# Attention's units: SyncE's transfers issued in the order of the source

## The chip, the core and the metric

The kernel runs on one core of a Trainium2 chip. The core has a matrix engine (TensorE, in the profile PE for matmuls and PEld for weight loads), a vector engine (VectorE, DVE), a scalar engine (ScalarE, ACT), GpSimd (POOL), and SyncE (SP), which here does nothing but issue DMA transfers. Each engine works through its own list of instructions in a fixed order. An instruction that has to wait for a semaphore holds up everything behind it on the same engine, and that holds for SP too: a transfer that is not yet allowed to start keeps all later transfers on SP from being issued.

The metric is the device time of one execution in microseconds, as the median of several executions.

## What is computed

One transformer layer: cross attention with 16 heads of 32 numbers over 4 batches of 1024 tokens, and then a feed-forward layer in which 32 experts with 4 sets each pick one token of every group of 32.

```
x = x + attention(layernorm(x), ctx, ctx)      # causal without the diagonal, 16 heads
x = x + ffn(layernorm(x))
    logits = group of 32 tokens @ controller + tie
    perm = (logits == max over the group)
    inner = relu(perm-dispatched tokens @ f1 + bias)
    out = perm-returned (inner @ f2)
```

All matmuls of the attention are in float32, except those with masks and maxima, which are in bfloat16.

## The kernel before, in words

The attention is cut into 16 units: `b` counts the 4 batches, `hc` the 4 groups of 4 heads, and u = 4b + hc. Each unit runs 12 steps (8 key blocks, of which the first half of the queries sees 4 and the second half 8). In every step TensorE makes scores of unit u + 1 for their row maxima (`score_piece`, L388 to L415), scores of unit u turned round for the exponential (`key_block`, L457 to L488), and weighs the values (`weigh_values`, L508). DVE reduces the maxima and adds one half of the softmax sums, ACT does the exponentials, POOL blanks the diagonal blocks (`affine_select`, L484) and adds the other half of the sums (L504). Matmuls for keys, queries, values and output rows of other units (L274, L288, L307, L348) are put in between by a small planner in the source (`slot`, `choose`, `one_part`), which counts costs while the program is being written out.

The order of PE, DVE, ACT and POOL is that of the source: the whole attention and the routing behind it stand in one `tc.manual_schedule` over these four engines (L1120 to L1127). SP is not in that set. Its transfers go into the order that a scheduler finds at compile time by its own estimate of when each may start; transfers with nothing to wait for are therefore issued early.

The transfers that matter here, all on SP:

- `xt` (L204, 1 MB): half a batch of x for the layernorm's statistics of the next batch. There is one buffer, so half 1 waits until DVE has measured half 0 (L211, L212).
- `stats_dram<-ln_both` (L216): mean and 1/sigma of 512 tokens, written to DRAM in pieces of 4 bytes. It waits for POOL's power (L215). In the source it stands ahead of the load of half 1 (L219, L220).
- `both<-stats_dram` (L235, 512 KB): these statistics, read back and spread over all partitions.
- `xnT` (L231, 2 MB): the next batch of x, turned round.
- `inverse_dram<-rd`, then four `inverse<-inverse_dram` (L553, L556): the reciprocal sums of one half unit go to DRAM and come back spread over the partitions; DVE multiplies by them (`atT`, L538).
- `xr<-in_x_dram` (L327, 256 KB, three buffers): the residual of one row of 128 tokens. POOL adds the bias to it (L328), DVE adds the output row (L354), and SP stores it (`x_dram<-xr`, L355). `o_step` for row t asks for the residual of row t + 1 (L343, L344).
- `ct` (L106, 1 MB) and the weights (L99).

Behind the units, from L773 on, the routing of tokens begins, still inside the same function: `roots` (L817) makes 1/sigma of the rows, one DVE instruction and six powers on POOL (L819, L822), and `last_row` (L800) makes the rows of the last batch, whose residuals POOL prepares through L328 as well. The feed-forward layer follows.

Of the kernel before, what the change touches and what calls it, by code (L numbers as in the profile page):

```python
# [37 lines left out]
def attention_phase(  # L38
# [29 lines left out]
    def given(engine, cost):  # L68
        engine[0] = max(engine[0], now[0] + 0.2) + cost
        return engine[0]  # L70

    def scores_free():
        return max(read[0], read[1]) + 0.1

    def scores_given(work, engine, cost):
        now[0] = max(now[0], scores_free()) + work
        for _ in range(2):
            read.popleft()
            read.append(given(engine, cost))


    opool = ctx.enter_context(tc.tile_pool(name="attn_out", bufs=1))
# [42 lines left out]
    def finish(*names):  # L125
        for name in names:
            if name in pieces_left:
                cost, work = pieces_left.pop(name)
                work()
                given(dve, cost)  # L130

    def beside(budget):
        while aside and budget > 0:
            name = aside.popleft()
            if name in pieces_left:
                budget -= pieces_left[name][0]
                finish(name)
# [250 lines left out]
    def score_piece(u, k):  # L388
        i, c0, n = pieces[k]
        kT, qT = ks[u], qs[u]  # L390
        half = i // 4
        if (u, half) not in nms:
            nms[u, half] = spool.tile([P, 2, 4, R], F32, tag=f"nm{half}", name=f"nm_{u}_{half}")
        nm = nms[u, half]
        scs = [
            ps_s.tile([P, 2, HS], F32, tag="sc", name=f"sc_{u}_{k}_{g}") for g in range(2)
        ]
        diag = c0 + n == (i + 1) * P
        for r in range(R):
            rr = ds(r * HD, HD)  # L400
            nc.tensor.matmul(  # L401
                scs[r // 2][:, r % 2, :n], lhsT=qT[rr, ts(i, P)], rhs=kT[rr, ds(c0, n)],
                start=True, stop=not diag,
            )
        if diag:
            for r in range(R):
                nc.tensor.matmul(  # L407
                    scs[r // 2][:, r % 2, ds(n - P, P)], lhsT=ident16,
                    rhs=masks[0 if i == 0 else 1], start=False, stop=True,
                )  # L410
        scores_given(LARGE * n / HS + (0.45 if diag else 0.1), dve, 0.15 + 2.1e-3 * n)
        for g in range(2):
            nc.vector.tensor_reduce(  # L413
                nm[:, c0 // HS, i % 4, ts(g, 2)], scs[g][:, :, :n], AX.X, ALU.max, negate=True
            )  # L415
# [41 lines left out]
    def key_block(u, k):  # L457
# [13 lines left out]
        for r in range(R):  # L471
# [3 lines left out]
                start=False, stop=True,  # L475
            )
        scores_given(1.07 * n / HS + 0.22, act, 0.2 + 1.8e-3 * n)
        prs[u, k] = []
        for g in range(2):
# [151 lines left out]
    def one_part():  # L631
        if open_step[0] is None:
            open_step[0] = choose(True)
        if not advance(open_step[0]):
            open_step[0] = None
# [132 lines left out]
    while soon or fill or open_step[0]:  # L768
        one_part()
    beside(1e9)  # L770
    units.close()

# [323 lines left out]
@with_exitstack  # L1098
def xattn_ffn(ctx: ExitStack, tc, x, xT, ctxT, wqT, wkT, wvT, bv, woT, bo, ctrl, f1, biasT, f2, tie, out):
    nc = tc.nc  # L1100
    B, S, D = x.shape
    N = B * S
    cpool = ctx.enter_context(tc.tile_pool(name="consts", bufs=1))
    dram = ctx.enter_context(tc.tile_pool(name="scratch", bufs=1, space=bass.MemoryType.DRAM))
    ident = cpool.tile([P, P], F32, tag="ident", name="ident")
    make_identity(nc, ident)
    ident16 = cpool.tile([P, P], BF16, tag="ident16", name="ident16")
    nc.vector.tensor_copy(ident16, ident)
    mhalf = cpool.tile([P, 4], F32, tag="mhalf", name="mhalf")
    nc.gpsimd.memset(mhalf, -0.5)  # L1110
    consts = (ident, ident16, mhalf)
    x2_dram = dram.tile([N, D], F32, tag="x2d", name="x2_dram")
    stats_dram = dram.tile([2 * B, 2, S // 2], F32, tag="statsd", name="stats_dram")
    inverse_dram = dram.tile([2 * B * (D // P) * P, P], F32, tag="inversed", name="inverse_dram")
    routed = (
        dram.tile([N, D], F32, tag="xn2d", name="xn2_dram"),
        dram.tile([N, P], F32, tag="permd", name="perm_dram"),
        dram.tile([P, N], F32, tag="permTd", name="permT_dram"),
    )
    engines = {  # L1120
        mybir.EngineType.PE, mybir.EngineType.DVE, mybir.EngineType.Activation, mybir.EngineType.Pool
    }
    with tc.manual_schedule(engines=engines):
        attention_phase(
            tc, consts, x, xT, ctxT, wqT, wkT, wvT, bv, woT, bo, ctrl, tie,
            x2_dram, stats_dram, inverse_dram, routed,
        )  # L1127
    ffn_phase(tc, consts, x2_dram, routed, f1, biasT, f2, out)


# [36 lines left out]
```

## Time and profile before

| | |
|---|---|
| three executions | 1470.87, 1472.08, 1479.79 us (median 1472.08) |
| the profiled execution | 1467.71 us; its span on the core is 1465.9 us |
| granted TensorE clock, mean | 0.979 |
| DVE, ACT, POOL busy | 63%, 34%, 33% of the span |
| DMA engines busy by SP's queue | 25.0% |

The profiled execution was about 4 us faster than the median. By stretch of the span, from the table of busy times:

| stretch, us | what runs | PE busy, us | POOL busy, us | granted clock |
|---|---|---|---|---|
| 0 to 40 | first loads, first unit's projections | 27.34 | 5.05 | 1.00 |
| 40 to 1110 | attention | 1050.70 of 1070 | 420.14 | 1.00 |
| 1110 to 1150 | the last unit's end, routing begins | 29.22 of 40 | 24.59 | 0.77 |
| 1150 to 1240 | routing | 82.03 of 90 | 12.57 | 0.94 |
| 1240 to 1466 | feed-forward layer | 204.08 of 226 | 24.23 | 0.95 |

A line of a timeline reads: start in us, duration in us, engine, source line, operation, what it writes and reads, how many, and in brackets how long the engine sat idle before it and what ended the wait. SPq lines are transfers being issued; their time is that of issuing, not of the data. The chain of waits is read from the last instruction back, each piece being what the next one had to wait for.

### The profile page before, as it was taken

How to read it: one execution, taken by the hardware profiler on the slowest of the kernel's cores; microseconds unless marked ns; L12 is line 12 of the kernel's file. 1: busy time of each engine (PE TensorE's matmuls, PEld its weight loads, DVE VectorE, ACT ScalarE, POOL GpSimd, SP SyncE). 2: the span in 40 equal slices, each digit the busy share in tenths (PEclk: the TensorE clock that was granted, in tenths of full speed). 3: DMA queues.
4: the chain of work that ended last, by engine and by line, in shares of the span. 5: the costliest groups of instructions: out<-in, count | busy, mean ns of one | idle time of the engine just before them, and what ended most of it. 6: DMA issues, size and time to landing. Idle time of an engine off the chain costs nothing.

```text
span 1465.9 us, 31695 instructions
## 1 busy us (share of the span) xinstructions
PE 1393.4 (95%) x13704; PEld 733.0 (50%) x13704; DVE 927.5 (63%) x1377; ACT 502.4 (34%) x785; POOL 486.6 (33%) x557
## 2 busy tenths in 40 slices
PE   6999999999899999999999999999998898997997
PEld 4344544445344533543535344434443555887887
DVE  3666777656558586666666766565674464576666
ACT  2033333323132223332322232323334123645664
POOL 1034344333425253434343434333356320000122
PEclk9999999999999999999999999999999797899999
DMA  8011202001230210011212000010112679657554
GB/s 298 26 48 35 77 24 67 20 1 41 57 105 30 89 53 10 11 56 40 86 44 62 30 19 11 10 38 10 39 39 76 222 245 327 178 164 235 184 165 146
DMA packets 96972, 125.25 MB, mean 85 GB/s; under 512 B 12992, under 2 KB 54336, under 8 KB 96704
## 3 DMA queue, kind: packets, MB, share of 16 engines
q1 hardware_dynamic: 94272, 114.84, 25.0%
q0 software_dynamic: 2560, 8.39, 1.9%
q8 instruction: 107, 1.75, 0.5%
q14 instruction: 33, 0.27, 0.1%
HBM read 91.78 MB, written 31.42 MB: 84 GB/s over the span
## 4 chain that ended last, share of the span: by engine, by line
PE 80%; issue 6%; DVE 6%; DMA 3%; POOL 2%; ACT 1%; SPq 0%; POOLq 0%; DVEq 0%; ACTq 0%
PE sc L401 12%; PE st L467 10%; PE av L517 9%; PE pq L288 8%; PE pk L274 8%; PE pv L307 8%; PE po L348 5%; PE pd L957 3%; PE sc L407 3%; DVE nm L413 2%; PE pi L976 2%; PE st L473 2%; PE po L808 2%; PE pl L845 2%; PE pd L543 2%
## 5 line engine op out<-in xcount | busy, mean ns | idle before, releaser
L413 DVE TENSOR_REDUCE nm<-sc 128x2 f32<-128x1024 f32 (+3 forms) x384 | 349.2, 951 | 264.3 <-PE sc L407 179.1
L481 ACT ACTIVATE pr<-st 128x1024 f32<-128x1024 f32 (+3 forms) x384 | 290.4, 808 | 584.3 <-PE st L473 563.1
L484 POOL TENSOR_SCALAR_AFFINE_SELECT pr<-pr 128x256 f32<-128x256 f32 x256 | 122.2, 487 | 383.5 <-ACT pr L481 381.4
L504 POOL TENSOR_TENSOR acc<-acc,pr 128x1024 f32<-128x1024 f32 (+3 forms) x128 | 209.4, 1636 | 93.3 <-ACT pr L481 85.6
L401 PE MATMUL sc<-kT,qT 32*128 32x512 f32 (+3 forms) x1536 | 206.3, 531 | 8.6 <-ACT pr L481 4.9
L467 PE MATMUL st<-qT,kT 32*128 32x512 f32 (+3 forms) x1536 | 191.1, 534 | 4.7 <-DVE nm L413 4.6
L517 PE MATMUL av<-pr,v 128*32 128x512 f32 (+3 forms) x1536 | 166.4, 501 | 7.8 <-POOL pr L484 4.3
L274 PE MATMUL pk<-ct,w_k 128*128 128x512 f32 x256 | 131.0, 629 | 9.9 <-DMA w_k<-in_wkT_dram 9.2
L307 PEld LDWEIGHTS pv<-w_v,ct 128*128 128x128 f32 x1024 | 119.5, 192 | 34.6 <-issue 24.7
L467 PEld LDWEIGHTS st<-qT,kT 32*128 32x128 f32 x1536 | 68.6, 183 | 127.6 <-issue 99.9
L401 PEld LDWEIGHTS sc<-kT,qT 32*128 32x128 f32 x1536 | 74.4, 183 | 115.4 <-issue 50.6
L504 DVE TENSOR_TENSOR acc<-acc,pr 128x1024 f32<-128x1024 f32 (+3 forms) x128 | 126.2, 986 | 9.2 <-POOL pr L484 8.9
L307 PE MATMUL pv<-w_v,ct 128*128 128x128 f32 x1024 | 131.4, 281 | 0.2 <-DMA w_v<-in_wvT_dram 0.2
L288 PE MATMUL pq<-xnT,w_q 128*128 128x512 f32 x256 | 127.3, 616 | 1.5 <-ACT xnT L194 1.5
L501 POOL TENSOR_TENSOR acc<-pr,pr 128x768 f32<-128x768 f32 (+1 forms) x32 | 66.7, 2085 | 161.5 <-ACT pr L481 161.5
L1078 POOL DMA_DIRECT2D out_dram<-xr x32 | 24.2, 757 | 238.8 <-DVE xr L1077 237.6
L348 PE MATMUL po<-w_o,atT 128*128 128x512 f32 x192 | 95.5, 616 | 0.0
L517 PEld LDWEIGHTS av<-pr,v 128*32 128x32 f32 x1536 | 32.0, 108 | 95.0 <-issue 67.2
L274 PEld LDWEIGHTS pk<-ct,w_k 128*128 128x128 f32 x256 | 43.9, 194 | 68.9 <-issue 55.0
L473 PE MATMUL st<-mxT,ones 32*128 32x512 bf16 (+3 forms) x768 | 74.6, 322 | 0.3 <-DVE mxT L444 0.3
L288 PEld LDWEIGHTS pq<-xnT,w_q 128*128 128x128 f32 x256 | 43.0, 189 | 52.9 <-issue 46.2
L967 DVE COPY disp<-pd 128x512 f32<-128x512 f32 x64 | 41.2, 686 | 33.0 <-PE pd L957 30.1
(101 smaller groups left out, 1499.7 us busy)
## 6 DMA issues: line engine op xcount, KB each, us to landing
ct<-in_ctxT_dram SPq DMA_DIRECT2D x8, 1024.0 KB, 5.1
xt<-in_x_dram SPq DMA_DIRECT2D x8, 1024.0 KB, 5.4
xr<-in_x_dram SPq DMA_DIRECT2D x32, 256.0 KB, 2.7
xn_dram<-x SPq DMA_DIRECT2D x8, 1024.0 KB, 5.7
xn<-xn_dram SPq DMA_DIRECT2D x8, 1024.0 KB, 5.5
f<-in_f_dram SPq DMA_DIRECT2D x16, 512.0 KB, 4.5
f<-in_f_dram SPq DMA_DIRECT2D x32, 256.0 KB, 5.9
xr<-x_dram SPq DMA_DIRECT2D x32, 256.0 KB, 4.7
```

Source lines behind the costliest of these rows:

```text
L274: nc.tensor.matmul(pk, lhsT=weights["k"][:, c, ts(hc, P)], rhs=cts[b, half][:, c, :], start=(c == 0), stop=(c == NC - 1),)
L288: nc.tensor.matmul(pq, lhsT=weights["q"][:, c, ts(hc, P)], rhs=xnTs[b][:, c, ts(half, HS)], start=(c == 0), stop=(c == NC - 1),)
L307: nc.tensor.matmul(pv[:, t, :], lhsT=cts[b, half][:, c, ts(t, P)], rhs=weights["v"][:, c, ts(hc, P)], start=(c == 0), stop=(c == NC - 1),)
L348: nc.tensor.matmul(po, lhsT=atTs[b * NC + c][:, ts(t, P)], rhs=weights["o"][:, c, :], start=(c == 0), stop=(c == NC - 1),)
L401: nc.tensor.matmul(scs[r // 2][:, r % 2, :n], lhsT=qT[rr, ts(i, P)], rhs=kT[rr, ds(c0, n)], start=True, stop=not diag,)
L413: nc.vector.tensor_reduce(nm[:, c0 // HS, i % 4, ts(g, 2)], scs[g][:, :, :n], AX.X, ALU.max, negate=True)
L467: nc.tensor.matmul(scs[r // 2][:, r % 2, :n], lhsT=kT[rr, ts(j, P)], rhs=qT[rr, ds(h * HS + q0, n)], start=True, stop=False,)
L473: nc.tensor.matmul(scs[r // 2][:, r % 2, :n], lhsT=ones16[rr, :], rhs=mxT[rr, ds(q0, n)], start=False, stop=True,)
L481: nc.scalar.activation(pr[:, :, :n], scs[g][:, :, :n], AF.Exp)
L484: nc.gpsimd.affine_select(out=d, in_=d, compare_op=ALU.is_ge, fill=0.0, base=0 if j == 0 else -1, pattern=[[0, 2], [P + 1, P]], channel_mu ...
L504: engine.tensor_tensor(acc, acc, pr[:, :, :n], ALU.add)
L517: nc.tensor.matmul(avs[u, h][rr, q0:], lhsT=vs[u][:, j, rr], rhs=pr[r // 2][:, r % 2, : HS - q0], start=(j == 0), stop=(j == last),)
```

## The change

SP joins the set of engines whose order is that of the source, for the units only; behind the units the routing stands in a `manual_schedule` of its own, without SP, as before.

```diff
@@ in attention_phase, ahead of the pools
+    compute = {
+        mybir.EngineType.PE, mybir.EngineType.DVE, mybir.EngineType.Activation, mybir.EngineType.Pool
+    }
+    ordered = ExitStack()
+    ordered.enter_context(tc.manual_schedule(engines=compute | {mybir.EngineType.SP}))
@@ behind the last unit
     beside(1e9)
+    ordered.close()
     units.close()
+    ctx.enter_context(tc.manual_schedule(engines=compute))
@@ in xattn_ffn
-    engines = {
-        mybir.EngineType.PE, mybir.EngineType.DVE, mybir.EngineType.Activation, mybir.EngineType.Pool
-    }
-    with tc.manual_schedule(engines=engines):
-        attention_phase(
...
+    attention_phase(
```

No instruction is added or taken away, but the built program differs in its order in three places.

PE and ACT keep every instruction where it was. SP's 380 transfers are the same ones, in another order up to the end of the units. Around the point where batch 3 is prepared (b is the batch whose rows are being finished):

```
before                                 after
xt half 1 (batch 3)                    stats_dram half 0
stats_dram half 0                      xt half 1 (batch 3)
both half 0                            inverse_dram, 4 inverse
inverse_dram, 4 inverse                stats_dram half 1
stats_dram half 1                      xr row 1
x_dram row 0, xr row 3                 x_dram row 0, ct, xr row 2
x_dram row 1, xr row 4                 x_dram row 1, xr row 3
x_dram row 2, inverse_dram, ...        x_dram row 2, inverse_dram, 4 inverse
xr row 5, xnT                          xnT, both half 0
```

So a residual's load stands one row later than before (that of row t + 2 behind the store of row t, where it was that of row t + 3), the loads of rows 1 and 2, which stood in the batch before, stand just ahead of their use, half 1 of `xt` stands behind the write of the statistics instead of ahead of it, and `both` stands behind `xnT`. The same holds for batches 1 and 2, where batch 1 has no rows to finish. At the start, `xt` half 1 now stands ahead of `w_o`, and `ct` of batch 1 and the first three residuals leave the front of the queue for the place of their use.

Third, the routing's instructions are no longer tied behind the units' by one common schedule, and the built program has some of them earlier. On DVE one instruction moves: `roots` (L819) stands behind the last row's moments of batch 2, ahead of the reciprocal of unit 15's first half, instead of behind the last `atT`. On POOL nine move: the residual of row 0 of batch 3 now stands ahead of unit 15's first diagonal block, and this is the stretch in the middle of unit 15:

```
before                                 after
acc (steps 4, 5)                       acc (steps 4, 5)
acc (step 6)                           rstd x6, xr row 1
acc (step 7)                           acc (step 6) 
affine_select (step 8)  ...            xr row 2
... acc (step 11)                      acc (step 7) 
xr row 0, rstd x6                      affine_select (step 8)  ...
xr row 1, xr row 2                     ... acc (step 11) 
```

More of the change, by code (lines that the diff above doesn't have):

```diff
@@ L1119, in xattn_ffn @@
     )
-    engines = {
-        mybir.EngineType.PE, mybir.EngineType.DVE, mybir.EngineType.Activation, mybir.EngineType.Pool
-    }
-    with tc.manual_schedule(engines=engines):
-        attention_phase(
-            tc, consts, x, xT, ctxT, wqT, wkT, wvT, bv, woT, bo, ctrl, tie,
-            x2_dram, stats_dram, inverse_dram, routed,
-        )
+    attention_phase(
+        tc, consts, x, xT, ctxT, wqT, wkT, wvT, bv, woT, bo, ctrl, tie,
+        x2_dram, stats_dram, inverse_dram, routed,
+    )
     ffn_phase(tc, consts, x2_dram, routed, f1, biasT, f2, out)
```

## The prediction

> **What bounds the kernel now.** I read the page first, then the chain of waits, then the waits of SP's queue, and then timelines of single places. TensorE is busy nearly all the time, and nearly all of the chain that ended last is its work:
>
> ```profile
> PE 1393.4 (95%) x13704; PEld 733.0 (50%) x13704; DVE 927.5 (63%) x1377; ACT 502.4 (34%) x785; POOL 486.6 (33%) x557
> PE 80%; issue 6%; DVE 6%; DMA 3%; POOL 2%; ACT 1%; SPq 0%; POOLq 0%; DVEq 0%; ACTq 0%
> ```
>
> So a better order of transfers can win little: in the attention (40 to 1110 us) PE is idle for 19 us in all. One place with a transfer in the chain is large:
>
> ```profile
> 356.79 11.34 DMA inverse_dram<-rd
> ...
> 369.44 3.18 DMA inverse<-inverse_dram
> ...
> 372.74 0.69 DVE atT L538
> ...
> 375.42 0.62 PE st L467
> ```
>
> A write of 64 KB takes 11.34 us here; the usual one takes 1.5 us (median of the DMA table). PE idles 4.62 us ahead of 375.42. Ahead of that write on SP stands the write of the statistics (issued at 356.11). What such a write does to its followers is seen best where nothing else moves:
>
> ```profile
> 677.77 0.38 SPq L216 DMA_DIRECT2D stats_dram<-ln_both  x1
> 682.12 0.34 SPq L355 DMA_DIRECT2D x_dram<-xr  x1
> 689.03 0.34 SPq L327 DMA_DIRECT2D xr<-in_x_dram  x1
> ```
>
> The load at 689.03 waits for the store of 682.12 to land (its buffer). That store takes 6.9 us instead of its usual 2.0, and ends 11.3 us after the statistics were issued. The other places agree: 356.11 to 368.13 is 12.0 us, and 395.58 to 408.00, the same pair in batch 2, is 12.4 us. So: what is queued behind a write of the statistics completes some 11.3 us after its issue. Each time the program before puts only writes, or nothing urgent, into that shadow. The change puts reads there that DVE and POOL wait for.
>
> **The change part by part.**
>
> *Start.* `xt` half 1 moves ahead of `w_o`. It is issued at 20.45 in both orders, as it waits for DVE's `xn`. DVE first reads it at 26.54, but PE meets its result only at 32.48, straight behind busy matmuls: a gain of some us there stays under PE. `w_o` is needed at the first output row, at 392.8, and `ct` and the early residuals at hundreds of us too: 0. If that cover were gone the loss would be one load, 5.4 us.
>
> *Residuals one row later.* Some 20 loads now follow the store two rows before. A load takes 2.7 us to land, rows are about 6 us apart, and the load no longer waits for a store that has just been issued (before: 2 to 4 us of SP each time). POOL adds the bias at a row's start (L328), so it may wait up to about 1 us and has slack at 39% load in this stretch. 0; bounds -1 and +3.
>
> *`xt` half 1 behind the statistics, batches 1 and 3.* Before, it is issued 1.5 us ahead of the statistics, and is in SBUF in time:
>
> ```profile
> 92.39 0.38 SPq L204 DMA_DIRECT2D xt<-in_x_dram  x1
> 93.91 0.37 SPq L216 DMA_DIRECT2D stats_dram<-ln_both  x1
> ```
> ```profile
> 99.81 0.68 DVE L211 BATCH_NORM_STATS2 ln_stats<-xt 128x6 f32<-128x512 f32 x1
> ...
> 102.04 0.96 DVE L550 RECIPROCAL rd<-pd 128x128 f32<-128x128 f32 x1 [1.33 <-PE pd L543]
> 103.50 2.35 DVE L413 TENSOR_REDUCE nm<-sc 128x2 f32<-128x1024 f32 x2 [0.50 <-PE sc L401]
> ```
>
> [...]The row of an undisturbed `xt` load is 5.4 us: issued at 94.3 it would land at 99.7, just in time, cost 0. [...]No read follows the statistics in this trace, so it can't show it. [...]With 1 MB to move, four times the store's, I put the landing at 12.0 us behind the issue: 105.9. DVE is then 6.1 us late; its idle 1.33 us absorbs some; the reductions at 103.50, which PE's next scores wait for, come 4.8 us late: **+4.8**. In batch 3 the statistics go at 642.60, `xt` lands at 654.6, DVE reads it at 649.92: 4.7 late, 0.6 absorbed ahead of the reciprocal at 652.73: **+4.1**. Bounds: 0 each by the row of the lone load; by full serial work (11.3 + 5.4 us) +9 each.
>
> *Batch 2.* The same, but there DVE waits for the inverse first. Write and loads of the inverse now stand behind `xt` and no longer with 512 KB of `both` between them: write complete at 356.11 + 12.2 = 368.3, last load issued 1.4 later, landing 2.0 later: 371.7 instead of 372.62: **-0.9**. Bounds -4.6 (the whole wait) and +4.
>
> *Residual of row 1 behind the second statistics, batches 2 and 3.* Before it was loaded long ahead. Now it completes as that store did, 11.3 us after the issue, at 689.1 in the copy shown above:
>
> ```profile
> 678.94 1.26 POOL L328 TENSOR_TENSOR xr<-xr,bo_sb 128x512 f32<-128x512 f32 x1
> 681.88 1.22 POOL L484 TENSOR_SCALAR_AFFINE_SELECT pr<-pr 128x256 f32<-128x256 f32 x2 [1.68 <-ACT pr L481]
> ```
> ```profile
> 684.21 1.20 DVE L504 TENSOR_TENSOR acc<-acc,pr 128x256 f32<-128x256 f32 x1
> ...
> 688.26 0.69 DVE L354 TENSOR_TENSOR xr<-po,xr 128x512 f32<-128x512 f32 x1 [2.08 <-PE po L348]
> ```
>
> POOL stands at L328 until 689.1, adds until 690.4, and only then blanks the diagonal of 681.88 (its first half done at 690.8). DVE's sum at 684.21 reads it: 6.6 late. DVE's 2.08 idle us ahead of L354 absorb part; PE's next row at 689.03 needs L354 to free its PSUM bank: **+4.4**, and the same again at 395.58: **+4.4**. Bounds: 0 by the lone load's 2.7 us, +6.6 by serial work.
>
> *POOL's own order in unit 15.* This needs no assumption on DMA:
>
> ```profile
> 1119.80 2.35 POOL L504 TENSOR_TENSOR acc<-acc,pr 128x1024 f32<-128x1024 f32 x1 [5.46 <-ACT pr L481]
> 1124.87 2.42 POOL L504 TENSOR_TENSOR acc<-acc,pr 128x1024 f32<-128x1024 f32 x1 [2.72 <-ACT pr L481]
> 1127.25 0.41 POOL L484 TENSOR_SCALAR_AFFINE_SELECT pr<-pr 128x256 f32<-128x256 f32 x1
> ...
> 1139.16 1.27 POOL L328 TENSOR_TENSOR xr<-xr,bo_sb 128x512 f32<-128x512 f32 x1
> 1144.98 6.17 POOL L822 TENSOR_TENSOR rstd<-rstd,mhalf 128x4 f32<-128x4 f32 x6 [4.55 <-DVE rstd L819]
> 1151.13 2.48 POOL L328 TENSOR_TENSOR xr<-xr,bo_sb 128x512 f32<-128x512 f32 x2
> ```
>
> The six powers and two residuals move ahead of the first two lines. DVE's last moments of batch 2 end at 1119.69, `rstd` at 1119.9, so on POOL: 6.2 of powers to 1126.1, residual to 1127.3, sum to 1129.7, residual to 1130.9, sum to 1133.4. The blanking of 1127.25 comes 6.1 us late, and from there to 1139 POOL is nearly without a gap and PE and DVE wait for it: +5.8. The residual of row 0, ahead of unit 15's first diagonal, lands at 1099.40 (its load is at 1096.88 either way), so the blanking of 1097.05 starts at 1100.7: 3.6 late, 2.8 after slack. Back comes the first power ahead of the routing's first tokens (1144.98 to 1146.03): -1.2. Sum **+7.4**; bounds 0 (POOL catches up) and +10.
>
> Sum: 4.8 + 4.1 - 0.9 + 4.4 + 4.4 + 7.4 = **+24.2 us**. Against the profiled execution's own 1467.7 that is 1491.9; the median of the runs shown stands 4.4 higher, so 1496.3, said as **1496 us**.
>
> **The rivals.**
>
> *The reads are not held* (the side of no change): a transfer into SBUF behind the statistics completes in its own 2.7 or 5.4 us. For it: [...]no read is shown late. Against it: [...]three late writes. Then both +4.4 and the +4.8 and +4.1 go, batch 2 gains 3 to 4.6, and POOL's 7.4 remains: +3 to +4, with the residuals' 1 us and less gain +8: 1475 to 1480, inside 1%. It decides where a read lands less than 6 us after the statistics' issue.
>
> *POOL absorbs its nine instructions*: the sums of unit 15 wait for ACT for 5.46 and 2.72 us, so some room is there. Against: the powers cannot start before 1119.9. Then 24.2 - 7.4 = +16.8: 1489.
>
> *Full serial work*: 9 + 9 + 6.6 + 6.6 + 4 + 7.4 = +42: 1514.
>
> *The order does what it is for*: SP's blocked head no longer delays others. All waits of DVE for the inverse are 18.9 us, 7 times, and most are the round trip itself; only the 4.6 us above reach PE. A gain over 1% is not in reach of that.
>
> **How the numbers follow.** Forecast 0.61, POOL absorbs 0.11, reads free 0.20, serial 0.06, a gain 0.02. One per cent, 14.7 us, is about what a measurement here tells from no change. Slower: the forecast, serial, and somewhat over half of the POOL case (1489 is at 1.14%), 0.73. Within 1%: reads free, the rest of the POOL case, 0.25. Faster: 0.02. The range goes from 1477, into the free reads, to 1504 (forecast with both `xt` landings 2 us later and 3 us more at rows); below and above it lie about 2 in 10.
>
> **What will show it.** SP's timeline: L204 directly behind L216 in batches 1 to 3. DVE: a wait of 5 to 6 us for DMA `xt` ahead of L211 near 100 us and near 655. POOL: a wait of about 10 us for DMA `xr` near 397 and 685, with PE's gap of 4 us behind it. Unit 15: `rstd` on POOL before the sums. It is wrong if those loads land within 6 us, or if PE has no gap behind unit 15's blanking.

## The result, and the profile after

| | before | after |
|---|---|---|
| median of the runs made together | 1471.5 us (1467.5 to 1479.8) | 1515.1 us (1514.7 to 1523.0) |
| ratio to before, 95% interval | | 1.030 (1.025 to 1.036) |
| profiled execution: time, span | 1467.7, 1465.9 us | 1523.0, 1521.3 us |
| mean granted TensorE clock of that execution | 0.979 | 0.961 |

The change costs 43.6 us, where 24.2 were forecast. The kernel before has only four runs here; beside the later experiments its medians are 1476.8 to 1479.2 us, so the cost may be nearer to 36 to 38 us, near the low end of the interval. The profiled execution after is 8 us longer than its median. Some 6.6 us come before 95 us, where nothing new waits and only the granted clock is lower: its record has two stretches of 6.83 us at half clock, from 61.67 and 75.33, which the profile before lacks. PE's longest pauses there are 0.35 and 0.79 us.

The page after, first its busy times and then the engines' shares of the chain that ended last:

```profile
PE 1414.3 (93%) x13704; PEld 740.3 (49%) x13704; DVE 928.4 (61%) x1377; ACT 502.6 (33%) x785; POOL 486.3 (32%) x557
PE 75%; issue 7%; DMA 6%; DVE 6%; POOL 4%; ACT 1%; SPq 0%; POOLq 0%; DVEq 0%; ACTq 0%
```

The work is the same (the counts are), the chain has moved: DMA from 3% to 6%, POOL from 2% to 4%. That PE is "busy" 21 us longer with the same 13704 matmuls already says that they ran slower.

Lines moved by 7: the load of `xt` is now L211, the write of the statistics L223, the residual's load L334, POOL's bias addition L335. SP's timeline in batch 1 (start, duration):

```profile
100.49 0.37 SPq L223 DMA_DIRECT2D stats_dram<-ln_both  x1
100.95 0.53 SPq L211 DMA_DIRECT2D xt<-in_x_dram  x1
```

and DVE's, with its idle time ahead of the instruction in brackets:

```profile
116.20 0.69 DVE L218 BATCH_NORM_STATS2 ln_stats<-xt 128x6 f32<-128x512 f32 x1 [9.71 <-DMA xt<-in_x_dram]
...
117.87 2.29 DVE L420 TENSOR_REDUCE nm<-sc 128x2 f32<-128x1024 f32 x2
```

The read is behind the write, as the order says. DVE waits 9.71 us for it, and the reductions of L420, which free TensorE's scores, stand behind. Whether the read was held or merely slow is seen in the view of the DMA over 98 to 120 us (40 slices of 0.55 us; the last rows give the size and the time from issue to landing):

```profile
DMA  0000005200004521351995422699963000000130
GB/s 0 0 0 0 0 0 5 2 0 0 0 0 22 26 22 15 30 19 11 63 22 15 11 11 34 153 317 384 361 246 138 26 11 0 0 0 0 29 90 0
...
xt<-in_x_dram SPq DMA_DIRECT2D x1, 1024.0 KB, 15.2
...
stats_dram<-ln_both SPq DMA_DIRECT2D x1, 4.0 KB, 11.6
```

The 4 KB of statistics (1024 pieces of 4 bytes) take 11.6 us to land. For some 7 us of that the 1 MB behind them crawls at 11 to 30 GB/s with single slices above it; its bulk moves at up to 384 GB/s when the write is nearly done. So the read's data itself waits. 15.2 us is 11.6 plus most of a load (5.4 us alone). Why the data waits, no run here shows.

In batch 2 the inverse stands behind both:

```profile
373.25 0.38 SPq L223 DMA_DIRECT2D stats_dram<-ln_both  x1
373.75 0.52 SPq L211 DMA_DIRECT2D xt<-in_x_dram  x1
374.31 0.50 SPq L560 DMA_DIRECT2D inverse_dram<-rd  x1
388.74 1.71 SPq L563 DMA_DIRECT2D inverse<-inverse_dram  x4
```

The read-back of the inverse waits for its write, which lands 15.4 us after the statistics' issue; the forecast had 12.2.

Row 1's residual in batch 3, on SP, then POOL, DVE and PE:

```profile
715.62 0.38 SPq L223 DMA_DIRECT2D stats_dram<-ln_both  x1
716.04 0.58 SPq L334 DMA_DIRECT2D xr<-in_x_dram  x1
```
```profile
727.74 1.26 POOL L335 TENSOR_TENSOR xr<-xr,bo_sb 128x512 f32<-128x512 f32 x1 [10.91 <-DMA xr<-in_x_dram]
728.96 0.77 POOL L491 TENSOR_SCALAR_AFFINE_SELECT pr<-pr 128x256 f32<-128x256 f32 x2
```
```profile
729.40 0.60 DVE L511 TENSOR_TENSOR acc<-acc,pr 128x256 f32<-128x256 f32 x1 [7.40 <-POOL pr L491]
```
```profile
724.09 1.98 PE L355 MATMUL po<-w_o,atT 128*128 128x512 f32 x4
...
731.92 3.78 PE L355 MATMUL po<-w_o,atT 128*128 128x512 f32 x4 [4.88 <-DVE xr L361]
```

This is the chain of the forecast link by link: POOL at its bias addition, the blanking behind it, DVE's sum, PE's row. The last line holds one more thing. Its four matmuls take 3.78 us, where those of the row before take 1.98. They run at about half speed. The view by windows shows it around the first stall (columns: window, length, busy time and instructions of PE, PEld, DVE, ACT, POOL; then the granted clock, DMA share, GB/s):

```profile
108.00:110.50 2.50, 2.50 (x30) 0.73 (x20) 0.00 (x0) 1.09 (x2) 1.33 (x1) 1.00 0.76 26
110.50:113.00 2.50, 0.91 (x4) 0.08 (x2) 0.00 (x0) 0.00 (x0) 1.02 (x1) 0.97 0.51 135
113.00:115.50 2.50, 0.00 (x0) 0.00 (x0) 0.00 (x0) 0.00 (x0) 0.00 (x0) 0.50 0.60 231
...
118.00:120.50 2.50, 1.41 (x6) 0.65 (x8) 2.50 (x3) 0.00 (x0) 0.00 (x0) 0.50 0.09 26
120.50:123.00 2.50, 2.50 (x16) 1.09 (x12) 1.21 (x2) 1.77 (x2) 0.00 (x0) 0.50 0.49 105
123.00:125.50 2.50, 2.50 (x18) 0.54 (x12) 1.61 (x3) 0.17 (x1) 2.19 (x1) 0.50 0.03 7
125.50:128.00 2.50, 2.50 (x21) 1.18 (x18) 2.47 (x4) 0.39 (x1) 0.16 (x1) 0.79 0.00 0
128.00:130.50 2.50, 2.50 (x22) 1.62 (x21) 0.16 (x1) 1.55 (x2) 0.81 (x1) 1.00 0.00 0
```

PE stops at 111.4 and starts again at 119.1. The granted clock is halved from 112.9 to 126.5, so PE works at half clock for 7.4 us. Each of the five stalls of the changed kernel ahead of unit 15 has such a tail; they last from 4.8 to 7.4 us. In the record of the granted clock the five slow stretches last 13.65, 10.24, 6.83, 10.24 and 6.83 us, which is four, three and two times 3.41, the shortest such stretch in this execution (near 1038 us). They begin 1.4 to 4.2 us after PE's last matmul (whose end is modelled in the profile). What sets these times, no run here shows.

Starts of the same matmul in the two profiled executions, compared in quiet places between the events, give what each event costs with its tail. The stall is the jump at the event itself:

| event | forecast | jump | with what follows it |
|---|---|---|---|
| before 95 us (clock alone, this execution) | 0 | | 6.6 |
| `xt`, batch 1 | 4.8 | 7.7 | 10.6 |
| `xt` and inverse, batch 2 | -0.9 | 2.3 | 2.0 |
| row 1, batch 2 | 4.4 | 5.0 | 7.9 |
| `xt`, batch 3 | 4.1 | 7.2 | 10.8 |
| row 1, batch 3 | 4.4 | 5.0 | 7.8 |
| 900 us to the end (unit 15) | 7.4 | | 9.8 |
| sum, us | 24.2 | | 55.4 |

55.4 is the difference of the two spans. Without the first row it is 48.8, and the medians differ by 43.6. The tails of the five stalls can be estimated from the clock as well: the half clock lasts for 30.5 us in all from where PE starts again, and for 5.3 us behind the one such stall before, which at half speed (the 3.78 us against 1.98 above) makes (30.5 - 5.3) / 2 = 12.6 us; the table has 39.1 - 27.2 = 11.9. The last row holds more than unit 15: 1.6 us come near 1038 us, where the clock dips once for 3.41 us, and 1.3 us in the feed-forward layer. Unit 15 itself, compared at 1090 and 1160 us of the kernel before, costs 7.0, with 20.5 us at half clock in both kernels.

### The profile page after: what moved, and what is told of

It is laid out like the page before. It is cut to its first block, busy times and chain, and to the rows that moved or that the text cites. A ratio compares the mean times of both kernels' runs of the same rounds, so it can differ in the third digit from the quotient of the medians.

```text
span 1521.3 us, 31670 instructions
## 1 busy us (share of the span) xinstructions
PE 1414.3 (93%) x13704; PEld 740.3 (49%) x13704; DVE 928.4 (61%) x1377; ACT 502.6 (33%) x785; POOL 486.3 (32%) x557
## 4 chain that ended last, share of the span: by engine, by line
PE 75%; issue 7%; DMA 6%; DVE 6%; POOL 4%; ACT 1%; SPq 0%; POOLq 0%; DVEq 0%; ACTq 0%
PE sc L408 11%; PE st L474 10%; PE pk L281 8%; PE pq L295 8%; PE av L524 8%; PE pv L314 7%; PE po L355 5%; PE pd L966 3%; DVE nm L420 3%; PE sc L414 2%; PE pi L985 2%; DMA xt<-in_x_dram 2%; PE st L480 2%; PE pl L854 2%; PE po L817 2%
## 5 line engine op out<-in xcount | busy, mean ns | idle before, releaser
L420 DVE TENSOR_REDUCE nm<-sc 128x2 f32<-128x1024 f32 (+3 forms) x384 | 349.3, 951 | 276.2 <-PE sc L414 184.6
L474 PE MATMUL st<-qT,kT 32*128 32x512 f32 (+3 forms) x1536 | 197.2, 545 | 21.3 <-DVE nm L420 21.2
L355 PE MATMUL po<-w_o,atT 128*128 128x512 f32 x192 | 99.2, 636 | 9.7 <-DVE xr L361 9.7
L1087 POOL DMA_DIRECT2D out_dram<-xr x32 | 24.2, 757 | 240.1 <-DVE xr L1086 238.9
L335 POOL TENSOR_TENSOR xr<-xr,bo_sb 128x512 f32<-128x512 f32 x32 | 40.9, 1281 | 90.5 <-DMA xr<-in_x_dram 63.5
```

What stands on the lines that cost most here:

```text
L355: nc.tensor.matmul(po, lhsT=atTs[b * NC + c][:, ts(t, P)], rhs=weights["o"][:, c, :], start=(c == 0), stop=(c == NC - 1),)
L420: nc.vector.tensor_reduce(nm[:, c0 // HS, i % 4, ts(g, 2)], scs[g][:, :, :n], AX.X, ALU.max, negate=True)
L474: nc.tensor.matmul(scs[r // 2][:, r % 2, :n], lhsT=kT[rr, ts(j, P)], rhs=qT[rr, ds(h * HS + q0, n)], start=True, stop=False,)
```

## The experiments

Each kernel was timed beside the kernel before on the same chip; ratios are to that. Times alone scatter by 1.3% here (the kernel before: 1467 to 1487 us in 29 runs made beside the last two kernels). Each run's span times its mean granted clock scatters by far less (1435 to 1443 in the same 29), so most of the scatter is clock. I use both: this product for the waits (a microsecond at half clock counts half in it, whether PE works or waits), and what is left, span times (1 - clock), for the clock. The end of a stall, which passes at half clock too, is therefore shared between the two.

**Undoing the parts, one by one and together.** First, `xt` half 1 ahead of the statistics:

```diff
             if i == 3:
...
+                if half == 0:
+                    load(1)
                 nc.sync.dma_start(
                     stats_dram[2 * b + half].rearrange("s (i p) -> p s i", p=P), mv
                 )
-                if half == 0:
-                    load(1)
```

> The changed kernel, but the load of xt half 1 is issued ahead of the first write of the statistics instead of behind it (batches 1 to 3); nothing else differs. Theory A (the read is held behind the statistics, and each stall of TensorE is followed by a stretch at a lower clock): the three stalls of 7.7, 2.3 and 6.7 us that the comparison of the traces shows go, and with them some 2 us each of slower clock: 1515 falls by 20 us (16 to 26), to about 1495; xt lands about 6 us after its issue; granted clock about 1.00 between 100 and 140 us. Theory B (the late xt costs what its stalls are, no clock loss): -16.7 at most. Theory C (the loss sits in the rows and in unit 15, the DVE wait for xt is absorbed): less than -6.

Second, row 1's residual with row 0's (POOL's bias addition for row 1 moves with it):

```diff
             if hc == 0:
                 load_residual(b - 1, 0)
+                if more:
+                    load_residual(b - 1, 1)
...
-        if ahead:
+        if ahead and ahead not in residuals:
             load_residual(*ahead)
```

> The changed kernel, but the residual of output row 1 is loaded together with that of row 0, ahead of the statistics of the next batch (batches 1 and 2's rows, loaded in batches 2 and 3); nothing else differs. Theory A: the two stalls of about 5 us at POOL's bias addition near 407 and 689 us go, with 2 to 4 us each of slower clock behind them: -14 us (-10 to -18). Theory B (stalls alone): -10. Theory C (POOL's wait is absorbed by slack): less than -4. POOL's wait for xr of about 10 us ahead of its bias addition should be gone.

Third, the four computing engines under one hand-written order around the whole phase, as before, and SP alone added within the units:

```diff
-    ordered.enter_context(tc.manual_schedule(engines=compute | {mybir.EngineType.SP}))
+    ordered.enter_context(tc.manual_schedule(engines={mybir.EngineType.SP}))
...
-    ctx.enter_context(tc.manual_schedule(engines=compute))
...
+    with tc.manual_schedule(engines=engines):
+        attention_phase(
```

> The changed kernel with SyncE in the new order, but with POOL and DVE in the order of the kernel before (nine instructions on POOL and one on DVE move back; SyncE's order is that of the changed kernel to the instruction). Theory A: unit 15's blanking is no longer behind the powers and two residuals: -6 us (-4 to -9), the sums of unit 15 on POOL at the distance they had before. Theory B (POOL catches up, the tail's loss comes from the transfers): within 2 us of the changed kernel.

All three:

> All three together: xt half 1 ahead of the statistics, row 1's residual with row 0's, POOL and DVE in the order before. What is left of the change is the order of the other transfers (w_o, ct, inverse and both, residuals one row later). If the three mechanisms are all of the loss and add up: 1515 - 20 - 14 - 6 = about 1475, within 5 us of the kernel before (1471.5). If the rest of SyncE's order costs something by itself: 1480 or more.

And the first two without the third, in a later set, so that POOL's order alone is left:

> The changed kernel with xt half 1 ahead of the statistics and row 1's residual with row 0's, and POOL and DVE left in the changed kernel's order: beside the run with all three undone (ratio 1.000 to the kernel before) only the nine instructions of POOL and one of DVE differ. Theory A (unit 15's blanking behind the powers and residuals costs some 8 to 10 us, stall and clock, as the profiles show): ratio to the kernel before 1.006, about 9 us. Theory B (POOL catches up; the run with POOL's order alone undone, 1.025 against 1.030, was noise): ratio 1.001 or less.

Measured, with the same comparison of matmul starts (us against the kernel before, by event):

```
                     ratio (95%)             batch 1  batch 2  row 1   batch 3  row 1   900 us
                                               xt     xt+inv   b. 2      xt     b. 3    to end
changed kernel       1.030 (1.025 to 1.036)   10.6     2.0     7.9     10.8     7.8      9.8
xt first             1.017 (1.010 to 1.023)    1.1     0.5     9.3      0.4     8.3      6.2
row 1 early          1.024 (1.017 to 1.030)   11.8     4.2     3.7     12.7     1.5      7.3
POOL as before       1.025 (1.020 to 1.030)   10.4     3.6     7.4     12.2     8.7     -1.5
first two            1.006 (1.003 to 1.008)    4.6     1.9     1.6      0.8     1.3      9.3
all three            1.000 (0.998 to 1.003)    1.5     0.5     1.9      0.0     1.5      2.4
```

Each edit takes away its own column, but for row 1 in batch 2, which keeps 3.7 of 7.9, and leaves or raises the other waits ahead of 900 us: this is what names the causes. By the ratios the three take back 20, 10 and 7 us of 1476, and 44 together. In span times clock it is 8.5, 3.8 and 2.5 us, and 22 together. Each time the singles fall short of the whole by 7 us. Scatter could make that in the times; in span times clock, which scatters less, it hardly does. Most of the columns for the untouched rows and `xt` are also larger in the singles than in the changed kernel. Why, stays open. In time, the first edit's 20 us can't tell theory A from B (16.7 at most); its granted clock can, at 1.00 from 100 to 140 us where the changed kernel has 0.82 and 0.84.

All three undone is the kernel before, within 0.3%, though some 25 of SP's instructions still stand elsewhere. So the rest of the new order (`w_o`, the residuals one row later, `ct`, `both`) costs nothing together that the times can tell. The profile of that run does show one small cost. The residual of row 2 stands behind the second statistics and 1 MB of `ct`, and in batch 2 it lands 12.0 us after its issue:

```profile
416.71 1.26 POOL L332 TENSOR_TENSOR xr<-xr,bo_sb 128x512 f32<-128x512 f32 x1 [11.16 <-DMA xr<-in_x_dram]
```
```profile
418.75 1.08 PE L547 MATMUL pd<-acc,pick 128*32 128x128 f32 x32 [1.64 <-DVE xr L358]
```

Batch 3 has the same, with 1.22 us on PE. In the columns these are the 1.9 and 1.5 us that stay at row 1.

POOL's order was not settled by its single run (the intervals overlap, and the median was 1515.0). The pair that differs in nothing else does: 1.006 against 1.000. The traces do too. The last column holds clock dips and scatter outside unit 15, but unit 15 itself, compared at 1090 and 1160 us of the kernel before, costs 7.0, 7.2, 6.7, -0.2, 6.7 and 0.0 us in the six lines of the table: nothing in the two runs with POOL's order as before, and about 7 us in the four others. In the run of the first two, POOL's timeline:

```profile
1134.90 6.70 POOL L833 TENSOR_TENSOR rstd<-rstd,mhalf 128x4 f32<-128x4 f32 x6 [5.65 <-DVE rstd L830]
1141.57 1.26 POOL L335 TENSOR_TENSOR xr<-xr,bo_sb 128x512 f32<-128x512 f32 x1
1142.79 2.78 POOL L511 TENSOR_TENSOR acc<-acc,pr 128x1024 f32<-128x1024 f32 x1
1145.54 1.26 POOL L335 TENSOR_TENSOR xr<-xr,bo_sb 128x512 f32<-128x512 f32 x1
1146.76 2.33 POOL L511 TENSOR_TENSOR acc<-acc,pr 128x1024 f32<-128x1024 f32 x1
1149.05 0.76 POOL L491 TENSOR_SCALAR_AFFINE_SELECT pr<-pr 128x256 f32<-128x256 f32 x2
```

and in the run of all three:

```profile
1127.03 2.35 POOL L508 TENSOR_TENSOR acc<-acc,pr 128x1024 f32<-128x1024 f32 x1 [5.50 <-ACT pr L485]
1132.03 2.43 POOL L508 TENSOR_TENSOR acc<-acc,pr 128x1024 f32<-128x1024 f32 x1 [2.65 <-ACT pr L485]
1134.41 0.41 POOL L488 TENSOR_SCALAR_AFFINE_SELECT pr<-pr 128x256 f32<-128x256 f32 x1
```

The two sums that waited for ACT in the second now wait behind powers and residuals, and no bracket is left between them: POOL has become the bound of this stretch.

**Is it the write, or its pieces?** The statistics written in the order in which SBUF holds them:

```diff
-                    stats_dram[2 * b + half].rearrange("s (i p) -> p s i", p=P), mv
+                    stats_dram[2 * b + half].rearrange("s x -> (s x)").rearrange(
+                        "(p s i) -> p s i", s=2, i=4), mv
...
-            xn = xnTs[b][:, c, ts(half, HS)]
+            xn = xnTs[b][:, c, ts(half, HS)].rearrange("q (i p) -> q i p", p=P)
+            st = both[half].rearrange("q s x -> q (s x)").rearrange(
+                "q (p s i) -> q s i p", s=2, i=4)
-            nc.vector.tensor_tensor(xn, xn, both[half][:, 0], ALU.subtract)
-            nc.vector.tensor_tensor(xn, xn, both[half][:, 1], ALU.mult)
+            nc.vector.tensor_tensor(xn, xn, st[:, 0], ALU.subtract)
+            nc.vector.tensor_tensor(xn, xn, st[:, 1], ALU.mult)
```

In the changed kernel:

> The changed kernel, SyncE's order untouched, but the statistics are written in the order that SBUF holds them: 128 pieces of 32 bytes instead of 1024 pieces of 4 bytes; DVE reads them back from both with a stride. Same 4 KB, same place in the queue. Theory A (the drain of 1024 tiny pieces holds what follows): the write lands after some 3 us instead of 11.6, xt in about 6 us instead of 15.2, the stalls for xt and for row 1's residual go with their clock tails; only unit 15's order stays: 1515 - 23 - 14 = about 1478. Theory B (any write to DRAM holds the reads behind it for some 11 us, whatever its pieces): 1515 as it was. If DVE reads a stride slower, its four normalisations per half grow from what they are and give some of it back.

In the kernel before:

> The kernel before, with the same contiguous write of the statistics. Theory A: the write of the inverse behind the second batch's statistics lands in 1.5 to 3 us instead of 11.3, so the stall of 4.6 us near 375 us goes, with 2 to 3 us of clock behind it: -5 to -8 us against the kernel before, about 1465. Theory B: no change.

The first measured 1483.5 us, 1.003 (1.000 to 1.006), with SP's order untouched. Its DMA over 99 to 112 us, the write and the read issued at the same distance as in the changed kernel:

```profile
GB/s 0 0 0 0 0 0 0 13 0 6 44 0 101 410 447 378 384 384 391 397 221 32 25 25 25 6 0 0 0 0 0 0 0 0 39 162 0 0 0 6
...
xt<-in_x_dram SPq DMA_DIRECT2D x1, 1024.0 KB, 6.6
...
stats_dram<-ln_both SPq DMA_DIRECT2D x1, 4.0 KB, 1.4
```

The same 4 KB land in 1.4 us instead of 11.6, and the read behind them takes 6.6 instead of 15.2. It is the pieces, not the place in the queue. (Their number and their size change together here, so which of the two counts is not shown.) Against the kernel before, the same comparison of matmul starts gives 0.0 for `xt` in batch 3 and at both row 1s, and 8.8 from 900 us to the end, with unit 15, which this edit does not touch. Batch 1 has 7.1 from about 240 us on, as the kernel before has with the same write (below), and batch 2 has -6.8, as the stall that the kernel before has there is gone too.

In the kernel before, the same edit gives 1470.8 us against 1479.2, 0.993 (0.991 to 0.996): 0.7% faster than the kernel that the study began with. Its own stall near 375 us is gone (window, PE's busy time, ..., clock 1.00 where the kernel before had 15.38 and 0.85):

```profile
360.00:380.00 20.00, 20.00 (x199) 10.76 (x198) 15.87 (x23) 6.99 (x9) 8.24 (x4) 1.00 0.29 97
```

The strided read has its price: DVE's two normalisations take 1.07 and 1.09 us each in the kernel before with this write, where they took 0.68 and 0.69 (the shortest of 24), and matmuls near 240 us come some 7 us late. The 8.3 us gained in batch 2 outweigh that.

**Would another queue help?** `xt` half 1 issued from ScalarE's queue, in the changed kernel:

```diff
-            nc.sync.dma_start(xt, x_t[b, half])
+            (nc.scalar if half else nc.sync).dma_start(xt, x_t[b, half])
```

> The changed kernel, but xt half 1 of batches 1 to 3 is issued from ScalarE's DMA queue instead of SyncE's; it is still issued behind the write of the statistics in time, as it waits for the same reads of its buffer. Theory A (the hold is one of SyncE's queue[...]): xt lands about 6 us after its issue, 1515 falls by about 20 us as in the run where the two are swapped. Theory B (the hold is in the DMA engines or the memory, whichever queue): xt still lands some 15 us after the statistics, 1515 stays. ScalarE loses about 0.4 us for the issue in either case.

1510.8 us, 1.022 (1.018 to 1.025). In batches 1 and 2 ScalarE issued the load 1.1 to 1.5 us ahead of the statistics, so those two say nothing. In batch 3 it came 0.4 us behind. The DMA view there (655 to 680 us):

```profile
GB/s 0 0 0 0 0 2 4 0 16 3 0 29 20 13 20 16 7 16 7 20 10 10 33 49 108 252 390 324 223 138 0 0 0 0 0 0 39 66 0 92
...
q10 hardware_dynamic: 528, 1.05, 32.8%
...
xt<-in_x_dram ACTq DMA_DIRECT2D x1, 1024.0 KB, 16.1
```

The same crawl on a queue of its own (q10), 16.1 us, and the event cost 12.1. It is one case, but there the hold is not one of SP's queue alone, and the other queue is no remedy.

**The clock by itself.** The kernel before, with eight pauses of DVE:

```diff
+    GAPS = (1, 2, 5, 6, 9, 10, 12, 13)
+    spare = wpool.tile([P, 6], F32, tag="spare", name="spare")
...
+                if k == 3 and u in GAPS:
+                    for _ in range(12):
+                        nc.vector.bn_stats(spare, bv_sb)
                 score_piece(u + 1, k)
```

> The clock by itself: the kernel before, SyncE's order untouched, with eight places (units 1, 2, 5, 6, 9, 10, 12, 13) where DVE takes 12 moments of a constant tile (12 x 0.68 = 8.2 us) ahead of a piece of the scores, so that TensorE waits for its scores to be read, some 5 us each time by the stalls for xt. Nothing of the transfers changes. Theory A (a stall of TensorE is followed by a stretch of lower clock that costs some 2 to 3 us more): time rises by about 8 x (5 + 2.5) = 60 us, while span times granted clock rises by only 40, and the granted clock falls from 0.975 to about 0.96; windows behind each place show 0.8 to 0.85. Theory B (the clock has nothing to do with stalls; the lower clock of the changed kernel comes from something else in it): time and span times clock rise by the same 40 us and the granted clock stays at 0.975.

1552.8 against 1479.2 us, 1.050 (1.047 to 1.053): 73.6 us. Span times clock rose by 41.4 (1439.2 to 1480.6), the rest from 36.9 to 72.1. Windows around one of the eight:

```profile
155.00:157.50 2.50, 0.49 (x8) 0.29 (x4) 2.40 (x4) 0.00 (x0) 0.00 (x0) 1.00 0.00 0
157.50:160.00 2.50, 0.00 (x0) 0.00 (x0) 2.36 (x5) 0.00 (x0) 0.00 (x0) 0.89 0.00 0
160.00:162.50 2.50, 0.64 (x8) 0.53 (x8) 2.50 (x3) 0.00 (x0) 0.00 (x0) 0.50 0.00 0
...
165.00:167.50 2.50, 2.50 (x7) 1.18 (x4) 2.38 (x3) 0.00 (x0) 0.41 (x1) 0.50 0.19 52
167.50:170.00 2.50, 2.50 (x4) 0.67 (x2) 0.80 (x4) 0.00 (x0) 0.00 (x0) 0.56 0.18 59
170.00:172.50 2.50, 2.50 (x22) 0.88 (x22) 0.00 (x0) 0.85 (x1) 0.00 (x0) 1.00 0.00 0
```

No transfer is concerned, and the clock falls as in the changed kernel. Theory B is out. A pause costs 5.2 us in span times clock and 4.4 in clock, which holds the slow end of the pause as well. By the starts of matmuls in the two profiles the eight pauses jump by 50 us and cost 74 with what follows, so about 3 us each are tail; theory A had 2.5.

**The change as it could have been made**: the source order of SP, POOL as before, and the statistics in 32-byte pieces (the third edit and the write in 32-byte pieces together).

> The change as it could have been made: SyncE's transfers of the units in the order of the source, POOL and DVE in the order before, and the statistics written in 128 pieces of 32 bytes. Theory A (the order of the source is neutral once nothing slow stands in it): the same as the kernel before with the same write, ratio 0.993 to the kernel before. Theory B (the order of the source frees SyncE's head and gains by itself): 0.990 or less. Theory C (the order of the source still costs, by loads issued late): 0.997 or more.

1471.7 against 1476.8 us, 0.997 (0.995 to 0.999). It is 0.3% faster than the kernel before. It lies at the edge of theory C, but its interval overlaps that of the scheduler's order with the same write (0.993, 0.991 to 0.996). The source order brings nothing that can be told; a small cost is not excluded.

## Why the prediction was wrong

The direction and the places named were right; the size was not: 24.2 us forecast, 43.6 measured, above the range. Two steps failed: the clock behind a stall, put at nothing (some 12 us), and the landing of what stands behind the statistics, put at 12.0 and 12.2 us where it took over 15 (some 9 us in `xt` and batch 2). By its steps:

- *What bounds the kernel; the 11.3 us shadow of the statistics.* Right, and the experiment on the pieces shows its cause, which the prediction did not have.
- *Start and residuals one row later, 0.* Right in the times, as all three undone is 1.000, and inside the bound of +3. But the residual of row 2 does stand in the shadow: PE waits 1.6 and 1.2 us for it in that run.
- *`xt` behind the statistics, +4.8 and +4.1.* To take the read as held, like the three late writes, was the right choice against the row of a lone load: in batch 1 it took 15.2 us and not 5.4. No read in the trace before had shown it; for reads it was the author's estimate. It was the term for the landing that failed: "I put the landing at 12.0 us behind the issue". Behind the issue of the statistics, from which the prediction counts, it was 15.7 and 15.4 us. The 12.0 leave 0.7 us for 1 MB beyond the 11.3 of a write behind the statistics; but the data crawls at 11 to 30 GB/s in most slices while the statistics drain, and its bulk moves, at up to 384 GB/s, only when they are nearly done. Jumps of 7.7 and 7.2 us instead of 4.8 and 4.1.
- *Batch 2, -0.9.* Wrong in sign for the same reason: the inverse stands behind 1 MB of `xt` that does not move yet. Its write lands after 15.4 us, not 12.2.
- *Row 1's residual, +4.4 twice.* Right: 5.0 and 5.0, by the same chain. In batch 2 the load lands 12.0 us behind the issue of the statistics, where 11.3 were forecast: 256 KB add little behind the drain.
- *POOL's order in unit 15, +7.4.* Right, in mechanism and size: 6.7 to 7.2 us across unit 15 in the four traces with this order (9.8 in the changed kernel's with what else lies behind 900 us), and about 8 us by the pair of runs (1.0056 less 1.0001, each known to 0.3%; 6 us in span times clock).
- *The term that was missing: the clock.* Nothing was put down for what follows a stall. The stalls before unit 15 jump by 27.2 us (forecast 16.8) and cost 39.1 with what follows them: some 12 us are clock, the largest single miss. In the medians, span times clock is 1461.3 after and 1438.4 before (15 runs beside the first experiments), +23; the clock's part is 53.0 and 37.0, +16 (with the slow ends of the stalls). Together that is 39 and not 43.6, as those 15 runs have a median of 1479.0 and not 1471.5. The profile of before had shown it, in the one place where it had such a stall ahead of unit 15:

```profile
371.50:374.00 2.50, 0.00 (x0) 0.00 (x0) 1.26 (x2) 0.00 (x0) 0.00 (x0) 0.97 0.11 33
374.00:376.50 2.50, 1.08 (x6) 0.57 (x8) 2.46 (x5) 0.00 (x0) 0.00 (x0) 0.50 0.00 0
376.50:379.00 2.50, 2.50 (x8) 0.72 (x5) 2.46 (x4) 1.38 (x2) 0.29 (x1) 0.50 0.00 0
```

Of the rivals, *reads not held* falls with the landings of 15 us, *POOL absorbs* with the pair of runs, *a gain* with the last experiment. *Full serial work* said 1514, and is nearest in time, but only in part for its reasons: the 1 MB load was nearly serial (15.7 of 16.7 us behind the statistics), the 256 KB one was not (12.0 of 14.0 in batch 2), and a large share of the rest was clock. That it came near is mostly luck.

## What to carry to other kernels

Before transfers are put in another order, look for the slow one among them, and ask what stands behind it in the new order: here 4 KB in 4-byte pieces held a megabyte for 15 us, and writing the same bytes in 32-byte pieces (1.4 us instead of 11.6) was worth more than any order tried here. A stall of a matmul engine that is else always busy is to be counted with its tail at half clock, which added 0.4 to 0.6 of it at four of the five stalls here, and about half in the kernel with pauses. An order given by hand to one engine moves others too: compare the order of every engine before the cost is summed.

## What the hardware showed that was not expected

- A DRAM write of 1024 pieces of 4 bytes takes 11.6 us (9.3 to 11.8 over the other landings in that trace), and while it drains, loads behind it crawl (11 to 30 GB/s in most slices against 384 after), in one case from another queue too (16.1 us to land). In 128 pieces of 32 bytes it takes 1.4 us with nothing ahead of it.
- After TensorE pauses of 4.8 to 7.7 us the granted clock stayed at 0.50 for 4.8 to 7.4 us of work. It fell 1.4 to 4.2 us after the last matmul. Eight such pauses cost 41 us in span times clock and 35 us in clock.
- The clock also fell without a stall: twice in the first 95 us of one execution, where PE's longest pause was 0.79 us, and not in the profile before, where PE has the same matmuls and the same pauses.
- Runs of one kernel differ by 1.3% in time and by 0.6% or less in span times granted clock: here, most of the scatter of a single core is its clock.
- A DVE operation on 512 values whose second operand is read with a stride of 32 bytes takes 1.07 us instead of 0.68.
